# Input loads in three pieces, and a single line for the transfers in the scheduler's model

## The chip, the cores and the metric

The kernel runs on one core of one Trainium2 chip. The metric is device time in microseconds (us) of one launch, as the median of several runs. A core has a matmul engine (PE, whose weight loads are shown as PEld), a vector engine (DVE), an activation engine (ACT), GpSimd (POOL) and a sync engine (SP); here SP issues nearly all plain transfers and POOL the accumulating ones. Each engine runs its own instructions in the order in which the program has them, and waits at semaphores for the others.

## The reference

The input x has 32 images of 96 channels and 56 x 56 pixels, in float32. Two layers follow one another.

```python
# layer 0: an inverted bottleneck with 576 hidden channels
h = relu(bn(einsum('oc,bchw->bohw', w1, x)))
h = relu(bn(dwconv3x3(h, wdw)))
x = x + bn(einsum('oc,bchw->bohw', w2, h))
# layer 1 on tokens t (3136 of 96 channels)
h = relu(bn(einsum('bnc,hc->bnh', ln(t), a_w1)))        # 192 hidden
X = fft(h, axis=tokens)
xr = relu(X.real * rd - X.imag * id + rb)
xi = relu(X.imag * rd + X.real * id + ib)
t = t + bn(einsum('bnh,ch->bnc', ifft(xr + 1j * xi).real, a_w2))
t = t + qlinear(relu(qlinear(ln(t), W1, b1)), W2, b2)   # 384 hidden, operands rounded to 5+2 bit floats
```

The Fourier transform over 3136 tokens is done as matmuls with constant matrices, in two steps of 56.

## The kernel before

**The work.** An image is taken in two halves of 28 rows. For each half, `load_half` (line 586) brings 29 rows of x, 96 x 1624 numbers, into one of three buffers `xs`. Then come five groups of hidden channels. `last_channels` does the last 64 wholly on PE. `unit` (line 600) does each of the other four groups of 128 channels:

- PE expands it (line 617) and ACT evicts it to `hs` (line 627).
- ACT begins the depthwise sum in `acc` (line 643) with one tap and puts another tap into a buffer `product` (line 659). In units 1 and 3 (`DOUBLE`), a second tap goes into a second `product`.
- DVE adds the other taps to `acc`, one instruction each (line 670).
- POOL issues an accumulating transfer (line 678) that adds `product` to `acc`; in the double units one that adds the second product to the first comes before it.
- ACT applies the Relu to `acc` (line 687, `finish`), when that transfer has landed.

`front` (line 865) projects the half to token layout on PE (line 883), stores it for later (`tdr<-xt`, line 942), normalizes it and does the first step of the Fourier transform; the result goes to memory (`ydr<-ya`, line 1064). `mid` (line 1072), twice an image, loads it back the other way round (`yb<-ydr`, line 1094, and the matrix `wb`, line 1083), does the second step, the mixing and half of the inverse, and stores `gdr<-gc` (line 1275). `back` (line 1291), four times an image, loads the matrix `wd`, `gd<-gdr` and `tt<-tdr`, finishes the inverse, and does the normalization (its square root is line 837) and the quantized layers.

**What sets the order.** The order of the instructions on every engine is found while the program is built, by a small simulation, `Plan.emit` (line 223). Every piece of work is a `Step` with an engine, a cost in us, the steps that it comes after, the buffers that it takes and gives back, and a rank. Whenever an engine of the simulation is idle, it takes the ready step of lowest rank and writes its instructions into the program. A step's results count as there `late` us after its end. For a transfer, `late` is a tuple, and `Plan.moved` (line 200) works out when it lands. Before the change, it starts 1.4 us after its issue and takes its size over a rate (170 GB/s for loads and stores, 200 GB/s for the accumulating transfers) and an extra (1.5 us for loads, 3.0 for stores, 0 for accumulates), and the time for which it overlaps transfers already under way comes on top:

```python
        start = now + 1.4
        end = start + size / rate
        wait = sum(max(0.0, min(end, b) - max(start, a)) for a, b in self.moving)
        self.moving.append((start, start + 1.3 * size / rate))
        return end + wait + extra - now
```

On the chip the order is kept as it was written, and each instruction waits for what it really needs. So the times that the simulation assumes decide where an instruction stands, not when it may run. If PE would be idle in the simulation too long, a filler matmul (line 1491) is put in.

Of the kernel before, what the change touches and what calls it, by code (L numbers as in the profile page):

```python
# [41 lines left out]
C = 96  # L42
HD = 576
S = 56
# [8 lines left out]
W = R * S  # L53
XW = XR * S
# [74 lines left out]
PACE = {"last": 3.023, "front": 0.4, "mid": 0.54, "back": 0.45}  # L129
CHAIN = 0.6  # L130

SPARSE = 0.75
FILLER = 0.23
FIRST = 15.0
# [2 lines left out]
AT = (3.0, 0.5)  # L137
# [17 lines left out]
class Plan:  # L155
# [12 lines left out]
    def __init__(self, free):  # L168
        self.free = dict(free)
        self.steps = []  # L170
        self.now = self.pace = 0.0
        self.window, self.share, self.slow = 0, {}, False
        self.moving = []
        self.filler, self.recent = None, []

    def stretched(self, now, work):
# [22 lines left out]

    def moved(self, now, moves):  # L200

        size, rate, extra = moves
        start = now + 1.4
        end = start + size / rate
        self.moving = [m for m in self.moving if m[1] > start - 20]
        wait = sum(max(0.0, min(end, b) - max(start, a)) for a, b in self.moving)
        self.moving.append((start, start + 1.3 * size / rate))
        return end + wait + extra - now

    def job(self, now, pace):  # L210

# [2 lines left out]
    def step(self, engine, cost, emit, after=(), take=(), give=(), late=None, rank=None):  # L214
        late = self.LATE.get(engine, 0.1) if late is None else late
        if rank is None:
            rank = self.now
            self.now += self.pace
        s = Step(engine, cost, emit, list(after), list(take), list(give), late, rank, len(self.steps))
        self.steps.append(s)  # L220
        return s
# [62 lines left out]
def tile_kernel(ctx: ExitStack, tc: tile.TileContext, d: dict, out: bass.AP):  # L284
    nc = tc.nc
    nimg = d["x"].shape[0]
    x = d["x"].rearrange("i c a b -> i c (a b)")
# [60 lines left out]
    xs_ring = [cst([C, XW], f"xs{j}") for j in range(3)]  # L348
# [18 lines left out]
    def load(queue, o, src):  # L367
        queue.dma_start(out=o, in_=src)
        return o
# [73 lines left out]
    s = scale_of(vec[:, 0, :], vec[:, 3, :], 128, NK + 1)  # L443

    ps = psum()
    for k in range(NK + 1):
        j, at = divmod(128 * k, 512)
# [4 lines left out]
            start=True,  # L452
# [5 lines left out]
    s = scale_of(vec[:, 4, :], vec[:, 7, :], 128, NK + 1)  # L458
# [70 lines left out]
    def ffn():  # L529
# [6 lines left out]
        for o, v, p, n in ((b1q, fb, 128, 3), (b2q, fc, C, 1)):  # L536
# [4 lines left out]
    xs, acc, ydr, gdr, tdr = {}, {}, {}, {}, {}  # L541
    base = [0, R - 1]
# [3 lines left out]
    plan = Plan(  # L546
        {
            "ps": 3, "pw": 1, "hs": 3, "acc": 7, "product": 3, "hl0": 1, "hl1": 1, "al": 2,
            "xt": 1, "norma": 2, "brief": 3, "xnT": 1, "z": 2, "ya": 1, "wb": 1, "yb": 2,
            "V": 2, "eo": 3, "real": 1, "wd": 1, "gd": 1, "tt": 2, "normf": 2, "u8": 1, "uT": 1,  # L550
            "h8": 1, "h16": 2, "y16": 1, "ydr": 4, "gdr": 3, "tdr": 4,
        }
    )
    step = plan.step
# [7 lines left out]
    def dve(n, fixed=0.13):  # L562
        return fixed + n / 960

    def read(n):
        return n * 4, 170e3, 1.5

    def written(n):
        return n * 4, 170e3, 3.0

    bands_set = [step("DVE", 1.2, bands(j), rank=2.0 + j) for j in range(2)]
    sets = []
    for n, (f, count) in enumerate(((second, 7), (attention, 6), (mixer, 21), (ffn, 4))):
        t = step("SP", 0.55 * count, fetch, sets[-1:], late=(150e3, 170e3, 1.5), rank=-20.0 + n)
        sets.append(step("DVE", 3.0, f, sets[-1:] + [t], rank=14.0 + 4 * n))
    second_set, mixer_set, *mid_set = sets

# [6 lines left out]
    loaded, ready, strips, taken = {}, {}, {}, {}  # L584

    def load_half(img, s):
        n = 2 * img + s

        def load():
            xs[img, s] = xs_ring[n % 3]  # L590
            at = base[s] * S
            nc.sync.dma_start(out=xs[img, s][0:C, :], in_=x[img, :, at : at + XW])

        after = []
        if n >= 3:
            i, t = divmod(n - 3, 2)
            after = [taken[i, t], strips[i, t, "hl"]]
        loaded[img, s] = step("SP", 0.1, load, after, late=read(C * XW), rank=16 * n - 24)

    def unit(img, s, k):  # L600
        n = (2 * img + s) * NK + k
        o = R * s - base[s]
        up = 1 - 2 * s
        u = {}

        def weight(dr, dc):
            at = 3 * (dr + 1) + dc + 1
            return wdw[:, k, at : at + 1]

        def expand(h):  # L610
            def mm():
                if h == 0:
                    u["hs"] = w2.tile([128, XR, S], F32, name="hs", bufs=3)
                u[h] = psum()
                for j in range(2):
                    at = (2 * h + j) * QW
                    nc.tensor.matmul(  # L617
                        u[h][:, j, 0:QW],
                        lhsT=w1T[:, 128 * k : 128 * (k + 1)],
                        rhs=xs[img, s][0:C, at : at + QW],  # L620
                        start=True,
                        stop=True,
                    )

            def evict():
                flat = u["hs"].rearrange("p r c -> p (r c)")
                nc.scalar.activation(  # L627
                    flat[:, 2 * h * QW : 2 * (h + 1) * QW].rearrange("p (j w) -> p j w", j=2),
                    u[h][:, :, 0:QW],
                    AF.Relu,  # L630
                    bias=b1[:, k : k + 1],
                )

            after = [loaded[img, s]] if h == 0 else [u["first"]]
            e = u["first"] = step("PE", pe(QW, 128, 4), mm, after, ["ps"] + ["hs"] * (h == 0), rank=4 * n + OFF[0] + h)
            return step("ACT", act(2 * QW, 1), evict, [e], [], ["ps"], rank=4 * n + OFF[0] + h)

        e = [expand(0), expand(1)]

        def begin():  # L640

            acc[img, s, k] = w1.tile([128, R, S], F32, name="acc", bufs=7)
            nc.scalar.activation(  # L643
                acc[img, s, k],
                u["hs"][:, o + up : o + up + R, :],
                AF.Identity,
                scale=weight(up, 0),
                bias=bd[:, k : k + 1],
            )

        def span(dr, dc):

            return max(0, -(o + dr)), min(R, XR - o - dr), max(0, -dc), S - max(0, dc)

        def product(dr):
            def f():
                ra, rb, _, _ = span(dr, 0)
                u["p", dr] = w1.tile([128, R, S], F32, name="product", bufs=3)
                nc.scalar.activation(  # L659
                    u["p", dr][:, ra:rb, :], u["hs"][:, ra + o + dr : rb + o + dr, :], AF.Copy, scale=weight(dr, 0)  # L660
                )

            return f

        def tap(dr, dc):
            def f():
                ra, rb, ca, cb = span(dr, dc)
                src = u["hs"][:, ra + o + dr : rb + o + dr, ca + dc : cb + dc]
                dst = acc[img, s, k][:, ra:rb, ca:cb]
                nc.vector.scalar_tensor_tensor(dst, src, weight(dr, dc), dst, ALU.mult, ALU.add)  # L670

            return f

        def add(to, dr):
            def f():
                ra, rb, _, _ = span(dr, 0)
                t = acc[img, s, k] if to is None else u["p", to]
                nc.gpsimd.dma_start(  # L678
                    out=t[:, ra:rb, :].rearrange("p r c -> p (r c)"),
                    in_=u["p", dr][:, ra:rb, :].rearrange("p r c -> p (r c)"),  # L680
                    accum_op=ALU.add,
                )

            return f

        def finish():
            nc.scalar.activation(acc[img, s, k], acc[img, s, k], AF.Relu)  # L687

        t = step("ACT", act(W, 2, 0.09), begin, e, ["acc"], rank=4 * n + OFF[1])
        c = [step("ACT", act(W, 1, 0.09), product(0), e, ["product"], rank=4 * n + AT[0])]  # L690
        rest = [q for q in TAPS[1:] if q != (up, 0)]
        if k in DOUBLE:

            rest.remove((-up, 0))
            c.append(step("ACT", act(W, 1, 0.09), product(-up), e, ["product"], rank=4 * n + AT[1]))
        for at, q in enumerate(rest):
            last = q == rest[-1]
            t = step("DVE", dve(W - 28, 0.16), tap(*q), [t] + c * last, [], ["hs"] * last, rank=4 * n + OFF[2] + at * 3.5 / len(rest))
        if k in DOUBLE:
            c = [step("POOL", 1.0, add(0, -up), c, [], ["product"], late=(W * 128 * 4, 200e3, 0.0), rank=4 * n + AT[1])]  # L700
        t = step("POOL", 1.0, add(None, 0), [t] + c, [], ["product"], late=(W * 128 * 4, 200e3, 0.0), rank=4 * n + 3)
        ready[img, s, k] = step("ACT", act(W, 0, 0.09), finish, [t], rank=4 * n + OFF[3])

    def last_channels(img, s):
# [854 lines left out]
```

## Time and profile before

| | |
|---|---|
| time, median of 3 runs | 4589.91 us (4589.24 to 4595.37) |
| span of the profiled execution | 4584.2 us |
| mean granted PE clock | 0.988 |
| DMA queue of SP: share of 16 engines, MB | 36.2%, 479.15 |
| DMA queue of POOL: share of 16 engines, MB | 34.4%, 304.64 |
| accumulate onto `acc`, from issue to landing, median | 8.0 us (256 of them) |
| accumulate onto `product`, the same | 10.1 us (128 of them) |
| input loads `xs` | 64, of 609 KB each |

The profile is one execution. An engine's busy time is the time in which it executes; time in which it waits is idle time, and a view of waits says which engine's instruction, or which transfer, ended each. A group of instructions is named by its line in the kernel and by what it writes and reads. Transfers are shown at their issue; for the accumulating ones the landing is shown as well.

### The profile page before, as it was taken

To read this page: it belongs to the slowest core of one execution; us is meant where nothing else is said; L and a number is where in the kernel's file an instruction comes from. 1 tells how busy PE (TensorE), PEld (TensorE's weight loads), DVE (VectorE), ACT (ScalarE), POOL (GpSimd) and SP (SyncE) were. 2 spreads that over 40 slices of the span, in tenths; PEclk is the share of its full clock that TensorE was granted. 3 is DMA by queue.
4 is the path that set the end of the run, shared out by engine and by line. 5 is a ranking of instruction groups with operands and counts; after the bars stand their busy time and mean duration, and the time that the engine had idled before them with its cause. 6 is when DMAs were issued, how large, how long until landed. Compare 5 with 4: busy or idle time off the path is not lost.

```text
span 4584.2 us, 88412 instructions
## 1 busy us (share of the span) xinstructions
PE 4405.4 (96%) x35128; PEld 3296.1 (72%) x35128; DVE 4330.6 (94%) x7053; ACT 4114.5 (90%) x5390; POOL 340.7 (7%) x403
## 2 busy tenths in 40 slices
PE   8989999999999999999999999999999999999998
PEld 5667776777777777777777777777777777777777
DVE  8998999999999999999999999999999999999967
ACT  5677999999999999999999999999999999999965
POOL 1000000000000000000000000000000000000000
PEclk9999999999999999999999999999999999999999
DMA  4666777767767777767777767777767777767663
GB/s 104 135 155 157 190 171 176 187 162 185 181 163 188 174 179 185 184 166 191 173 176 185 183 163 188 174 176 183 187 162 188 174 174 190 179 165 191 168 170 107
DMA packets 390993, 789.44 MB, mean 172 GB/s; under 512 B 135696, under 2 KB 236628, under 8 KB 390580
## 3 DMA queue, kind: packets, MB, share of 16 engines
q1 hardware_dynamic: 335028, 479.15, 36.2%
q0 software_dynamic: 55488, 304.64, 34.4%
q8 instruction: 276, 4.52, 0.4%
q14 instruction: 137, 1.12, 0.1%
q10 hardware_dynamic: 64, 0.01, 0.0%
HBM read 286.38 MB, written 192.68 MB: 105 GB/s over the span
## 4 chain that ended last, share of the span: by engine, by line
PE 48%; ACT 22%; DVE 16%; DMA 8%; issue 4%; POOLq 0%; ACTq 0%; POOL 0%; SPq 0%; DVEq 0%
PE pw L883 11%; DVE acc L670 10%; PE ps L617 9%; DMA acc<-product 7%; PE ps L1005 4%; PE ps L1123 4%; PE ps L755 3%; PE ps L1036 3%; ACT product L659 3%; ACT hs L627 2%; ACT acc L687 2%; ACT acc L643 2%; PE ps L1329 2%; ACT h L1410 2%; ACT h L1395 2%
## 5 line engine op out<-in xcount | busy, mean ns | idle before, releaser
L670 DVE SCALAR_TENSOR_TENSOR acc<-hs,wdw,acc 128x1540 f32<-128x1540 f32 (+2 forms) x1664 | 2970.3, 1792 | 26.6 <-ACT acc L643 20.8
L617 PE MATMUL ps<-xs,w1T 96*128 96x406 f32 x2048 | 819.8, 523 | 24.6 <-ACT h L1395 16.7
L883 PEld LDWEIGHTS pw<-w2T,acc 128*112 128x112 f32 x7168 | 754.3, 178 | 62.1 <-issue 36.4
L883 PE MATMUL pw<-w2T,acc 128*112 128x96 f32 x7168 | 790.8, 264 | 4.5 <-ACT acc L687 4.5
L659 ACT ACTIVATE product<-hs,wdw 128x1568 f32<-128x1568 f32 (+1 forms) x384 | 613.8, 1599 | 21.6 <-DMA product<-product 20.9
L617 PEld LDWEIGHTS ps<-xs,w1T 96*128 96x128 f32 x2048 | 368.2, 194 | 261.7 <-issue 174.0
L627 ACT ACTIVATE hs<-ps,b 128x812 f32<-128x812 f32 x512 | 481.5, 941 | 51.2 <-PE ps L617 46.8
L687 ACT ACTIVATE acc<-acc 128x1568 f32<-128x1568 f32 x256 | 387.5, 1514 | 90.9 <-DMA acc<-product 85.1
L678 POOL DMA_DIRECT2D acc<-product x256 | 222.7, 870 | 3193.9 <-DVE mf L859 781.6
L643 ACT ACTIVATE acc<-hs,bd,wdw 128x1568 f32<-128x1568 f32 x256 | 437.0, 1707 | 0.3
L755 PE MATMUL ps<-hl,band 128*64 128x385 f32 (+3 forms) x3072 | 416.1, 495 | 0.3 <-ACT hs L627 0.3
L1005 PE MATMUL ps<-watt,xnT 97*120 97x192 f32 x1792 | 345.3, 337 | 60.9 <-DVE V L1152 59.6
L1005 PEld LDWEIGHTS ps<-watt,xnT 97*120 97x120 f32 x1792 | 299.0, 187 | 125.3 <-DVE V L1152 65.6
L1123 PEld LDWEIGHTS ps<-wb,yb 112*128 112x128 f32 x3528 | 297.3, 164 | 66.5 <-issue 20.9
L1395 ACT ACTIVATE h<-ps 128x784 f16<-128x784 f32 x384 | 319.6, 835 | 25.8 <-PE ps L1383 22.0
L1350 ACT ACTIVATE u<-tt,mf,rf 112x96 fp8e5<-112x96 f32 x812 | 312.3, 460 | 16.6 <-DVE mf L859 16.5
L1123 PE MATMUL ps<-wb,yb 112*128 112x112 f32 x3528 | 321.8, 271 | 4.4 <-ACT hs L627 2.6
L1410 ACT ACTIVATE h<-h 128x784 fp8e5<-128x784 f16 x348 | 301.9, 867 | 14.9 <-DVE h L1401 14.8
L755 PEld LDWEIGHTS ps<-hl,band 128*64 128x64 f32 (+1 forms) x3072 | 151.9, 134 | 198.9 <-issue 164.2
L1152 DVE SCALAR_TENSOR_TENSOR sb<-ps,cw,V 128x784 f32<-128x784 f32 x192 | 197.0, 1026 | 31.1 <-ACT V L1136 25.4
L1018 ACT ACTIVATE z<-ps 120x768 f32<-120x768 f32 (+1 forms) x256 | 182.3, 725 | 44.9 <-PE ps L1005 44.9
L1036 PE MATMUL ps<-z,wa 56*64 56x384 f32 (+1 forms) x2048 | 217.5, 496 | 0.3
(171 smaller groups left out, 6663.3 us busy)
## 6 DMA issues: line engine op xcount, KB each, us to landing
acc<-product POOLq DMA_DIRECT2D x256, 784.0 KB, 8.0
product<-product POOLq DMA_DIRECT2D x128, 756.0 KB, 10.1
yb<-ydr SPq DMA_DIRECT2D x252, 294.0 KB
wd<-in_wd_dram SPq DMA_DIRECT2D x128, 349.1 KB
wb<-in_wb_dram SPq DMA_DIRECT2D x63, 686.0 KB
ydr<-ya SPq DMA_DIRECT2D x256, 168.0 KB
xs<-in_x_dram SPq DMA_DIRECT2D x64, 609.0 KB
tdr<-xt SPq DMA_DIRECT2D x64, 588.0 KB
```

The costliest lines, as they stand in the source:

```text
L617: nc.tensor.matmul(u[h][:, j, 0:QW], lhsT=w1T[:, 128 * k : 128 * (k + 1)], rhs=xs[img, s][0:C, at : at + QW], start=True, stop=True,)
L627: nc.scalar.activation(flat[:, 2 * h * QW : 2 * (h + 1) * QW].rearrange("p (j w) -> p j w", j=2), u[h][:, :, 0:QW], AF.Relu, bias=b1[:, k ...
L643: nc.scalar.activation(acc[img, s, k], u["hs"][:, o + up : o + up + R, :], AF.Identity, scale=weight(up, 0), bias=bd[:, k : k + 1],)
L659: nc.scalar.activation(u["p", dr][:, ra:rb, :], u["hs"][:, ra + o + dr : rb + o + dr, :], AF.Copy, scale=weight(dr, 0))
L670: nc.vector.scalar_tensor_tensor(dst, src, weight(dr, dc), dst, ALU.mult, ALU.add)
L687: nc.scalar.activation(acc[img, s, k], acc[img, s, k], AF.Relu)
L755: nc.tensor.matmul(pv[:, :, ca:cb], lhsT=band[rows, j, dc + 1, 64 * o : 64 * o + 64], rhs=H[rows, q : q + 7, ca + dc : cb + dc], skip_grou ...
L883: nc.tensor.matmul(u["pw"][0:SK, t, n % 4, 0:C], lhsT=src[rows, (G * t + n) * SK : (G * t + n + 1) * SK], rhs=rhs, skip_group_check=True, **k,
L1005: nc.tensor.matmul(pv[0:PK, q - a, 0:HA], lhsT=xnT[:, q, 0:PK], rhs=watt, start=True, stop=True,)
L1123: nc.tensor.matmul(o, lhsT=lhsT, rhs=u["wb"][:, G * s + q, :], start=True, stop=True)
L1395: nc.scalar.activation(u["h", c].rearrange("p (j w) -> p j w", j=2), u["H", c][:, :, 0:n], AF.Copy)
L1410: nc.scalar.activation(u["h8"][:, c, :], u["h", c], AF.Copy, saturate=False)
```

## The change

It has two parts. First, an input load is cut by columns into three transfers of 560, 560 and 504 columns; in the simulation each of the second and third is issued when the one before it has landed. (The very first load stays whole.) The units may begin when the last piece has landed. It is meant to keep a large load from standing in the way of other transfers. Second, the simulation's model of transfers is replaced: all of them pass through one line at 225 GB/s, each begins at the earliest 1.0 us after its issue and when the one before it is through, and it counts as landed 0.5 us later, or 1.3 us later for the accumulating ones. With other landing times, the simulation may write another order for every engine. The work itself, its instructions and its buffers are the same except for the pieces.

```diff
+RATE = 225e3
+HARD = 0.5
+SOFT = 1.3
...
-        self.moving = []
+        self.moving = 0.0
...
     def moved(self, now, moves):
 
-        size, rate, extra = moves
-        start = now + 1.4
-        end = start + size / rate
-        self.moving = [m for m in self.moving if m[1] > start - 20]
-        wait = sum(max(0.0, min(end, b) - max(start, a)) for a, b in self.moving)
-        self.moving.append((start, start + 1.3 * size / rate))
-        return end + wait + extra - now
+        size, extra = moves
+        self.moving = max(self.moving, now + 1.0) + size / RATE
+        return self.moving + extra - now
+
+    def trickle(self, load, cuts, size, after, take, **k):
+
+        for n, (a, b) in enumerate(zip(cuts, cuts[1:])):
+            after = [self.step("SP", 0.1, load(a, b), after, take if n == 0 else [], late=(4 * size * (b - a), HARD), **k)]
+        return after[0]
...
     def read(n):
-        return n * 4, 170e3, 1.5
+        return n * 4, HARD
 
     def written(n):
-        return n * 4, 170e3, 3.0
+        return n * 4, HARD
...
-        t = step("SP", 0.55 * count, fetch, sets[-1:], late=(150e3, 170e3, 1.5), rank=-20.0 + n)
+        t = step("SP", 0.55 * count, fetch, sets[-1:], late=(150e3, HARD), rank=-20.0 + n)
...
-        def load():
-            xs[img, s] = xs_ring[n % 3]
-            at = base[s] * S
-            nc.sync.dma_start(out=xs[img, s][0:C, :], in_=x[img, :, at : at + XW])
+        def load(a, b):
+            def f():
+                xs[img, s] = xs_ring[n % 3]
+                at = base[s] * S
+                nc.sync.dma_start(out=xs[img, s][0:C, a:b], in_=x[img, :, at + a : at + b])
+
+            return f
...
-        loaded[img, s] = step("SP", 0.1, load, after, late=read(C * XW), rank=16 * n - 24)
+        cuts = [0, XW] if n == 0 else [0, 560, 1120, XW]
+        loaded[img, s] = plan.trickle(load, cuts, C, after, [], rank=16 * n - 24)
...
-            c = [step("POOL", 1.0, add(0, -up), c, [], ["product"], late=(W * 128 * 4, 200e3, 0.0), rank=4 * n + AT[1])]
-        t = step("POOL", 1.0, add(None, 0), [t] + c, [], ["product"], late=(W * 128 * 4, 200e3, 0.0), rank=4 * n + 3)
+            c = [step("POOL", 1.0, add(0, -up), c, [], ["product"], late=(W * 128 * 4, SOFT), rank=4 * n + AT[1])]
+        t = step("POOL", 1.0, add(None, 0), [t] + c, [], ["product"], late=(W * 128 * 4, SOFT), rank=4 * n + 3)
```

## The prediction, made before the changed kernel was run

> **What bounds the kernel now.** I read the page first, for the share of each engine.
>
> ```profile
> span 4584.2 us, 88412 instructions
> PE 4405.4 (96%) x35128; PEld 3296.1 (72%) x35128; DVE 4330.6 (94%) x7053; ACT 4114.5 (90%) x5390; POOL 340.7 (7%) x403
> ```
>
> Three engines are nearly full. PE's 4405.4 us hold 207.1 us of filler matmuls (line 1491), which do no work of the kernel, so DVE is the fullest engine: it has 4330.6 us of work, none of which the change touches, and 4584.2 - 4330.6 = 253.6 us of idle time. Any gain must come out of that. The view by windows says where it lies.
>
> ```profile
> core 0: us, PE busy (x) PEld busy (x) DVE busy (x) ACT busy (x) POOL busy (x), PEclk, DMA share, GB/s
> 0.00:400.00 400.00, 354.48 (x2531) 260.83 (x2532) 356.76 (x418) 261.17 (x267) 39.01 (x57) 0.94 0.61 137
> 400.00:4286.00 3886.00, 3770.90 (x30228) 2808.63 (x30228) 3743.65 (x6012) 3650.64 (x4837) 293.84 (x337) 0.99 0.73 178
> 4286.00:4585.00 299.00, 280.06 (x2377) 226.63 (x2373) 230.24 (x625) 202.72 (x287) 7.89 (x9) 1.00 0.55 143
> ```
>
> DVE idles 43.2 us at the start (18.5 of them before the first tap), 142.4 in the steady part and 68.8 at the end. The steady part repeats: 24 pairs of input loads take 138.1 us each, so an image has some 5 us of DVE idle time. The list of waits says on whom.
>
> ```profile
> ACT acc L687 <- DMA acc<-product: 85.1, 40, 5.1
> DVE rf L853 <- ACT sdf L837: 55.4, 62, 3.1
> ```
>
> DVE never waits for a DMA outside the set-up; it waits for ACT. ACT waits for a DMA 40 times at line 687, the Relu on a depthwise unit after its accumulating transfer. Those 40 have a pattern: from 400 us on there is one to an image, at the same place. Image 14, by the timelines of SP, POOL, ACT and DVE:
>
> ```profile
> 2009.31 0.43 SPq L592 DMA_DIRECT2D xs<-in_x_dram  x1
> 2010.76 0.32 SPq L942 DMA_DIRECT2D tdr<-xt  x1
> 2016.00 0.28 SPq L1301 DMA_DIRECT2D wd<-in_wd_dram  x1
> ```
>
> ```profile
> 2017.10 0.86 POOL L678 DMA_DIRECT2D acc<-product  x1 [14.74 <-DVE da L834]
> 2018.20 0.86 POOL L678 DMA_DIRECT2D product<-product  x1 [0.24 <-ACT product L659]
> ```
>
> ```profile
> 2026.64 1.51 ACT L687 ACTIVATE acc<-acc 128x1568 f32<-128x1568 f32 x1 [1.93 <-DMA acc<-product]
> 2028.05 0.19 ACT L837 ACTIVATE sdf<-wf 112x7 f32<-112x7 f32 x1
> ```
>
> ```profile
> 2028.28 0.20 DVE L853 RECIPROCAL rf<-sdf 112x7 f32<-112x7 f32 x1 [1.25 <-ACT sdf L837]
> ```
>
> The reader is to see a chain of four: a 609 KB input load and a 588 KB store go out 6 to 8 us ahead of an accumulate; the accumulate takes 9.52 us; ACT, in order, stands 1.93 us at line 687; the square root behind it comes late and DVE stands 1.25 us. Over all accumulates onto acc in the trace: 55 of the 64 input loads have one issued 6 to 9 us after them, and these take 9.4 us on average, while those 16 to 25 us after a load take 6.7 and those 25 to 40 us after it 6.0. Summing DVE's gaps within a DMA stall of ACT and the 3 us after it gives 41.8 us in the steady part, 156 us of it; at the rate elsewhere (2.7%) 4.2 us would be there. So the stalls cost DVE about 37.6 us, 1.3 us an image.
>
> **What the Trainium skill says.** "DMA: Bandwidth & Descriptors", section "Queues, rings and completion order", has each DMA engine go round the queues with work, a packet at a time. The trace agrees: between 2018 and 2027 us the packets of the accumulates and of the sync queue run side by side, 113 and 208 KB in the microsecond from 2019. The same page, "Issuing engines are not separate DMA queues", says that all issuers' transfers interleave on the same 16 engines, so a piece of an input load is still in an accumulate's way; only when it is put in changes. "PSUM — Partial Sum Buffer", section "Engine vs sequencer instructions", has the ACT and DVE queues as strict first-in first-out; the 1.93 us at line 687 that become 1.25 us of DVE show it.
>
> **The change, part by part.**
>
> 1. *Input loads in pieces.* 63 of 64 loads become three: 126 more transfers. Issuing one takes SP 0.43 us, so 126 x 0.43 = 54 us in all, 1.7 us an image. SP stands for hundreds of us on single lines (807.8 us for line 1314 alone), which hides it. Behind a waiting piece stand the other loads and stores of SP; pieces two and three wait for no buffer, only for their place in the order and one of SP's eight completion semaphores, which comes round after eight transfers (4584 us / 1770 of them x 8 = 20.7 us), against landings of 3 to 14 us. The rows shrink from 6,496 to 2,240 or 2,016 bytes; a 6,496-byte packet takes 247 to 384 ns in the trace, the nearest short one, 2,304 bytes, 93 ns, so three are some 280 ns, read from the trace's packet records: no cost. The last piece lands perhaps 10 us later than the one load did; a buffer of the ring of three comes free at rank 16n - 22.6 (the end of front n-3) and is first read at 16n - 4.5: 18 of the 32 ranks of an image, 18/32 of 138 us = 78 us. Hidden.
>
> 2. *What pieces bring.* When the accumulate of 2017.10 goes out, the sync queue still has work from the four yb loads, the input load, the store and wd. With pieces, the store goes ahead of the second and third, 409 KB. At the 250 GB/s moved there, 409 KB are 1.6 us, if neither has been issued by then, and 0.8 us if one has. ACT's stall of 1.9 us becomes 0.3 to 1.1 us.
>
> 3. *The order's model of DMA.* The order of all engines is fixed when the program is built, so a landing that is assumed wrongly becomes a wait. I put the old and the new formula over the transfers of the trace, in their order of issue. The trace's landing less the formula's, medians: product into product +3.1 us old, +1.0 new; product into acc +0.6 and +0.2; stores of ya, out and xt -2.5, -3.3 and -3.7 old, -0.2, -0.3 and -1.1 new; wb -2.1 and +0.3. So the new model is closer for most, and the spread is less for acc (1.3 to 1.0 us). The order will put line 687 of the double units later, behind the landing, and give back ya and the three "brief" tiles 2.5 to 3.3 us sooner. It gets worse for loads that PE waits for: yb +0.1 to +0.9, wd +0.6 to +1.9, gd -0.1 to +1.9. PE waits for none of them now, the buffers being filled long ahead, so I cost this at nothing.
>
> 4. *The start.* ACT's DMA stalls ahead of 400 us are 45 us, but SP is fetching weights and DVE waits mostly for the fill; I take 5 us of the 43.2.
>
> Sum: two thirds of 37.6 us (halfway between 0.3 and 1.1 us left of 1.9) is 25 us; 5 us at the start; 5 us of the other 100 us of steady idle time for buffers given back sooner, an estimate. 4590 - 35 = 4555 us.
>
> **The rivals.**
>
> *The whole order gets better.* Besides the stall, half of the 100 us goes: 4590 - 37 - 35 = 4518 us, with DVE at 98% in the steady part. For it: waits on ACT are what a wrong order makes. Against: the largest of them (line 837's and 1136's results) come from ACT's own costs, which stay as assumed.
>
> *Hidden or only moved.* Pieces two and three come out while the accumulate moves and take turns with it, so it lands as late as before: 4590 us. For it: the bytes are the same, and the trace shows the queues side by side. Against: the backlog ahead of the accumulate is shorter.
>
> *Slower: a new wait takes its place.* A piece now follows each landing, so two or three accumulates in a half may meet one, where one in an image stalled; or the shorter assumed landings of yb, wd and gd put a PE step ahead of its data. A stall such as today's costs 1.3 us x 31 = 40 us; one more than now gives 4630 us, and half a one 4610. For it: any change of assumed times deals the whole order anew, and 93% of ACT's and 96% of DVE's steady time is full. Against: the formulas fit better.
>
> **How the numbers follow.** Forecast 0.45 (4535 to 4575 us); better order 0.16; hidden 0.15, of which 0.03 falls to faster and 0.02 to slower; new wait 0.24. Faster by over 0.2% (under 4580.7): 0.45 + 0.16 + 0.03 = 0.64; within: 0.10; slower: 0.24 + 0.02 = 0.26. The range runs from 4505, a little beyond the better order, to 4625, most of one new stall an image; about 0.05 lies below and 0.12 above.
>
> **What would show it.** Right: the wait of ACT line 687 for the DMA falls from 85 us to under 40; no accumulate 6 to 9 us after an input piece takes over 9 us as a rule; product into product lands as before, near 10 us; DVE's steady idle time is 105 to 120 us at an unchanged 4330 us of work; the image's period is near 137 us. Wrong: line 687's wait as long as before at another place in the image; PE waiting for yb, wd or gd; DVE's waits for lines 837, 1136 and 1437 grown while the DMA wait shrank, which would mean that the new order, not the transfers, sets the time.

## The result and the profile after

The changed kernel takes 4565.05 us (median of 4 runs, 4560.63 to 4573.17) against 4589.57 us before: a ratio of 0.9948, 95% interval 0.9929 to 0.9968. That is 24.5 us or 0.5% faster; forecast were 35 us, to 4555, with a range of 4505 to 4625.

First the page of the changed kernel: the span, and the busy time of each engine.

```profile
span 4558.5 us, 88951 instructions
PE 4409.0 (97%) x35334; PEld 3306.1 (73%) x35334; DVE 4330.5 (95%) x7053; ACT 4118.9 (90%) x5390; POOL 341.6 (7%) x403
```

DVE's work is what it was, 4330.5 us against 4330.6. The whole difference of the spans, 4584.2 - 4558.5 = 25.7 us, is idle time of DVE. PE's work is not quite the same: the simulation wrote another number of filler matmuls, 1588 where 1382 stood, and these are the 206 more on PE. The view by windows of the changed kernel:

```profile
core 0: us, PE busy (x) PEld busy (x) DVE busy (x) ACT busy (x) POOL busy (x), PEclk, DMA share, GB/s
0.00:400.00 400.00, 367.23 (x2684) 270.43 (x2685) 365.96 (x430) 273.50 (x281) 39.32 (x58) 0.97 0.64 142
400.00:4286.00 3886.00, 3790.56 (x30483) 2827.55 (x30483) 3755.65 (x6049) 3663.87 (x4849) 296.14 (x339) 1.00 0.74 178
4286.00:4585.00 299.00, 251.20 (x2171) 208.14 (x2169) 208.85 (x576) 181.51 (x262) 6.18 (x7) 0.97 0.50 130
```

In the steady window DVE idles 3886.0 - 3755.7 = 130.3 us, where it was 142.4. Windows at fixed times cut the two programs at different work, so I also summed DVE's idle time up to equal amounts of DVE work: of the 25.6 us won, 13.6 come up to 400 us of work (images 1 to 3), 8.1 between 400 and 4100 us of work, and 3.9 in the end. An image takes 137.8 us, against 138.1 (images 4 to 30). The steady part has hardly moved. The waits of the changed kernel:

```profile
DVE h L1411 <- ACT h L1405: 54.0, 69, 6.4
ACT acc L697 <- DMA acc<-product: 41.9, 44, 2.7
DVE rf L863 <- ACT sdf L847: 22.6, 29, 2.4
```

Line numbers are 10 higher than before (7 for the input load). The wait that was to shrink did: ACT at its Relu waits 41.9 us for the accumulate where it waited 85.1, and DVE for the square root 22.6 where it waited 55.4. But other waits grew: DVE now waits 54.0 us at the quantized layer (44.5 before), and 16.7 us for PE in a step of `back`, where 5.8 stood. And the accumulates themselves land no sooner. The page's list of DMA issues, with the median time to landing last (8.0 and 10.1 us before):

```profile
acc<-product POOLq DMA_DIRECT2D x256, 784.0 KB, 8.9
product<-product POOLq DMA_DIRECT2D x128, 756.0 KB, 10.6
```

The old stall is also still there, once in three images. SP's timeline of the changed kernel near 2130 us, then POOL's, ACT's and DVE's:

```profile
2128.62 0.30 SPq L952 DMA_DIRECT2D tdr<-xt  x1
2128.97 0.43 SPq L599 DMA_DIRECT2D xs<-in_x_dram  x1
2133.86 0.28 SPq L1311 DMA_DIRECT2D wd<-in_wd_dram  x1
2134.18 0.31 SPq L599 DMA_DIRECT2D xs<-in_x_dram  x1
```

```profile
2134.71 0.86 POOL L688 DMA_DIRECT2D acc<-product  x1 [14.97 <-ACT pj L1245]
```

```profile
2144.39 1.51 ACT L697 ACTIVATE acc<-acc 128x1568 f32<-128x1568 f32 x1 [1.85 <-DMA acc<-product]
```

```profile
2146.03 0.20 DVE L863 RECIPROCAL rf<-sdf 112x7 f32<-112x7 f32 x1 [1.22 <-ACT sdf L847]
```

It is the chain of before with nearly the same sizes (1.85 and 1.22 us here, 1.93 and 1.25 before). The store went ahead of the piece as forecast, but the next piece goes out 0.5 us before the accumulate, which takes 9.66 us.

### The profile page after: what moved, and what is told of

It is laid out like the page before. It is cut to its first block, busy times and chain, and to the rows that moved or that the text cites. A ratio compares the mean times of both kernels' runs of the same rounds, so it can differ in the third digit from the quotient of the medians.

```text
span 4558.5 us, 88951 instructions
## 1 busy us (share of the span) xinstructions
PE 4409.0 (97%) x35334; PEld 3306.1 (73%) x35334; DVE 4330.5 (95%) x7053; ACT 4118.9 (90%) x5390; POOL 341.6 (7%) x403
## 4 chain that ended last, share of the span: by engine, by line
PE 39%; DVE 23%; ACT 22%; DMA 10%; issue 5%; SPq 0%; POOL 0%; POOLq 0%; DVEq 0%; ACTq 0%
DVE acc L680 15%; PE pw L893 11%; DMA acc<-product 8%; PE ps L627 6%; ACT acc L653 3%; ACT acc L697 3%; PE ps L1015 3%; ACT product L669 2%; PE ps L1133 2%; PE ps L1046 2%; PE ps L1339 2%; ACT hs L637 2%; ACT u L1360 2%; DVE sb L1162 1%; DMA gdr<-gc 1%
## 5 line engine op out<-in xcount | busy, mean ns | idle before, releaser
L627 PE MATMUL ps<-xs,w1T 96*128 96x406 f32 x2048 | 807.0, 517 | 22.8 <-ACT h L1405 9.1
L697 ACT ACTIVATE acc<-acc 128x1568 f32<-128x1568 f32 x256 | 387.5, 1514 | 47.9 <-DMA acc<-product 41.9
L1501 PE MATMUL pw<-ident 128*128 128x128 f32 x1588 | 228.5, 283 | 4.7 <-ACT xt L943 4.7
L1501 PEld LDWEIGHTS pw<-ident 128*128 128x128 f32 x1588 | 206.9, 195 | 30.2 <-issue 16.3
```

The source lines that it names most:

```text
L627: nc.tensor.matmul(u[h][:, j, 0:QW], lhsT=w1T[:, 128 * k : 128 * (k + 1)], rhs=xs[img, s][0:C, at : at + QW], start=True, stop=True,)
L1501: nc.tensor.matmul(pw[:, 0, 4 * C :], lhsT=ident, rhs=ident, start=False, stop=False, skip_group_check=True)
```

## The experiments

The theories. **A**: the transfers matter. Pieces clear the way for the accumulate behind an input load, and a closer model avoids waits. **B**: the new landing times write a better order, and the pieces are hidden. **C**, formed after the first four runs: any small change of the assumed times writes the whole order anew, as cards are dealt anew (below such an order is called a deal), and the deal sets the time. Medians and ratios to before, in the order of the runs:

| run | us | ratio, 95% interval |
|---|---|---|
| the changed kernel | 4565.05 | 0.9948, 0.9929 to 0.9968 |
| e1 pieces, old model | 4548.50 | 0.9914, 0.9900 to 0.9928 |
| e2 new model, whole loads | 4484.38 | 0.9774, 0.9761 to 0.9788 |
| e3 changed order, whole loads | 4570.18 | 0.9960, 0.9948 to 0.9973 |
| e4 order of before, little input | 4527.73 | 0.9870, 0.9855 to 0.9884 |
| e5 changed kernel at 220 GB/s | 4496.41 | 0.9790, 0.9772 to 0.9808 |
| e6 changed kernel at 230 GB/s | 4625.91 | 1.0074, 1.0052 to 1.0096 |
| e7 e2 at 220 GB/s | 4635.40 | 1.0092, 1.0074 to 1.0111 |
| e8 e2 at 230 GB/s | 4655.87 | 1.0137, 1.0119 to 1.0155 |
| e9 order of before, pieces | 4600.63 | 1.0024, 1.0016 to 1.0032 |
| e10 order of e2, pieces | 4482.43 | 0.9765, 0.9753 to 0.9778 |
| e11 changed kernel, two pieces | 4476.28 | 0.9756, 0.9743 to 0.9769 |
| e12 changed kernel, accumulates 0.5 us later | 4507.71 | 0.9822, 0.9809 to 0.9836 |

**Each part alone (e1, e2).** In e1 `moved` and its numbers stay as before and the load is cut; against the kernel before:

```diff
+            after = [self.step("SP", 0.1, load(a, b), after, take if n == 0 else [], late=(4 * size * (b - a), 170e3, 1.5), **k)]
...
-        loaded[img, s] = step("SP", 0.1, load, after, late=read(C * XW), rank=16 * n - 24)
+        cuts = [0, XW] if n == 0 else [0, 560, 1120, XW]
+        loaded[img, s] = plan.trickle(load, cuts, C, after, [], rank=16 * n - 24)
```

> Three pieces, with the old model of landings (170 GB/s, 1.5 us). Theory A (the pieces clear the way for the accumulate that follows an input load): the wait of ACT for the accumulate at the Relu falls from 85 us to under 45, and the time to about 4565 us. Theory B (what counts is the new order that the new landing times write, and the pieces are hidden): another order without the better landing times, so no gain to be counted on: 4580 to 4620 us.

In e2 the model is the new one and the load stays whole; against the changed kernel:

```diff
-        cuts = [0, XW] if n == 0 else [0, 560, 1120, XW]
+        cuts = [0, XW]
```

> The new model of landings with whole input loads. Theory A: the accumulates that follow a whole load still take over 9 us and stall ACT; the wait at the Relu is near 80 us and the time 4580 to 4595 us. Theory B: the gain is here, 4555 to 4575 us, with the start (the first three images) shorter by some 13 us of DVE idle time as in the changed kernel.

Each part alone is faster than both together: 41 us and 105 us won, 24.5 together. A's sign for e1 came out (the Relu's wait is 26.2 us), but its e2 didn't: whole loads, and the wait is 31.0 us. B fares no better: e2 was 71 us faster than B's range, its start is 8 us shorter and not 13, and the changed kernel, which is e2 with pieces and the order that comes of them, is 81 us slower than e2. Effects that don't add up like this speak against both. The waits of e2:

```profile
DVE h L1411 <- ACT h L1405: 84.6, 97, 6.4
ACT acc L697 <- DMA acc<-product: 31.0, 24, 5.4
```

Most of DVE's idle time in e2's steady part (58 us) sits in one kind of wait, at the quantized layer. The waits for the square root (2.9 us, 55.4 before) and for the begun sum (3.4, 20.8 before) are all but gone. The view by windows of e2, columns as above, has DVE idle for 70.5 of 3850 us:

```profile
400.00:4250.00 3850.00, 3800.91 (x30565) 2815.36 (x30564) 3779.54 (x6110) 3687.07 (x4906) 297.66 (x343) 1.00 0.76 182
```

**The same order, other transfers (e3, e4).** e3 keeps the order of the changed kernel on all engines and moves the whole load in the first piece's place:

```diff
-                nc.sync.dma_start(out=xs[img, s][0:C, a:b], in_=x[img, :, at + a : at + b])
+                if a == 0: nc.sync.dma_start(out=xs[img, s][0:C, :], in_=x[img, :, at : at + XW])
```

> Every engine's order exactly as in the changed kernel, but the whole input load is issued in the place of the first piece and the places of the other two are empty. It isolates what the pieces do on the chip. Theory A: the wait of ACT at the Relu rises from 42 us to 65 or more, and the time by 10 to 25 us, to 4575 to 4590. Theory B: the time stays within 5 us of the changed kernel's 4565.

It takes 4570.18 us, 5.1 more than the changed kernel, with intervals that overlap: on the chip, three pieces or one is no difference to be told here. The Relu's wait is not 65 us:

```profile
ACT acc L697 <- DMA acc<-product: 45.7, 41, 5.5
```

So A fails here, and B, which allowed 5 us, holds but for a hair. e2 and e3 both issue whole loads, and 86 us lie between them: what differs is the order, with the fillers in it (1286 and 1588).

e4 keeps the order of before and takes the load away, nearly:

```diff
-            nc.sync.dma_start(out=xs[img, s][0:C, :], in_=x[img, :, at : at + XW])
+            nc.sync.dma_start(out=xs[img, s][0:C, 0 : XW if n < 3 else S], in_=x[img, :, at : at + (XW if n < 3 else S)])
```

> The order of before exactly; from the fourth half image on, an input load brings only the first 56 of 1624 columns (the rest of the half is computed on old columns). It takes the load out of the accumulate's way altogether and so measures the most that the contention can cost. Theory A: the wait at the Relu falls from 85 us to under 30 and the time by about 38 us, to 4552. Theory B: the accumulate still waits for the store and the other loads, or DVE's time comes back in other waits: less than 15 us, 4575 to 4590.

62 us won, more than A's 38, although the Relu's wait fell only to 46.3:

```profile
ACT acc L687 <- DMA acc<-product: 46.3, 37, 4.6
DVE rf L853 <- ACT sdf L837: 23.0, 45, 2.7
```

The windows of before, then of e4, leave DVE 141.9 and 91.5 us idle of 3850:

```profile
400.00:4250.00 3850.00, 3734.90 (x29913) 2780.21 (x29913) 3708.09 (x5964) 3615.78 (x4791) 291.26 (x334) 0.99 0.73 178
400.00:4250.00 3850.00, 3769.25 (x30332) 2804.24 (x30334) 3758.55 (x6057) 3662.66 (x4856) 295.45 (x339) 1.00 0.72 172
```

So in the order of before the load's traffic does cost: DVE waits 23.0 us for the square root where it waited 55.4. Whether pieces spare any of it is what e9 asks.

But the accumulates themselves hardly gained. Those issued 6 to 9 us after a load take 8.8 us on average in e4, where they took 9.4, though the load now brings 56 columns of 1624. The trace of before shows what else is beside them: all 55 run together with an accumulating transfer of product into product, and of the 64 accumulates 16 to 40 us after a load only two do. The accumulates more than 40 us after any load take 9.3 us too: 10.0 with such a transfer beside them, 8.5 without. So the prediction's comparison (9.4 us against 6.7 and 6.0) set accumulates that have a second accumulating transfer beside them against accumulates that have none, and put the difference down to the load. About 0.6 us of it is the load's bytes. No run moved the transfer of the products.

**The deal (e5 to e8).** One number is changed, the assumed rate, to 220 or 230 GB/s, with pieces (e5, e6) and with whole loads (e7, e8):

```diff
-RATE = 225e3
+RATE = 220e3
```

> The changed kernel with an assumed rate of 220 instead of 225 GB/s: nothing changes but the order that the simulation writes. Theory A (the time follows from how well the model fits the transfers): 2% of the rate is within the fit's error, so 4565 us within 10. Theory C (the order is dealt anew by any small change of the assumed times, and the deal sets the time): it lands anywhere in 4490 to 4620 us, and differs from 4565 by 15 us or more.

> The changed kernel with an assumed rate of 230 GB/s. Theory A: 4565 us within 10. Theory C: anywhere in 4490 to 4620 us, by 15 us or more from 4565, and not on one line with the run at 220.

> The new model with whole loads (4484 us at 225 GB/s), with 220 GB/s. Theory A: within 10 us of 4484, as whole loads would be better than pieces under this model. Theory C: 4484 was a lucky deal: 4510 to 4600 us.

> The new model with whole loads, with 230 GB/s. Theory A: within 10 us of 4484. Theory C: 4510 to 4600 us, at the upper end, since the simulation's own end with this rate is 58 us later than with 225 (4532 against 4474).

Theory A fails in all four runs. Theory C holds in the main: all four lie far outside A's 10 us. Its ranges were too narrow, though: e6, e7 and e8 are slower than C had them (4620 and 4600 at most). With pieces, 220, 225 and 230 GB/s give 4496, 4565 and 4626 us, which is close to one line, against C's forecast; with whole loads they give 4635, 4484 and 4656, which is not. A change of 2% in one assumed number moves the time by 61 to 171 us, while all instructions but the fillers are the same. The changed kernel less the one with whole loads, at the three rates, is -139, +81 and -30 us, which is no effect of pieces. The waits of e8, the slowest:

```profile
DVE h L1411 <- ACT h L1405: 100.4, 58, 6.4
ACT acc L697 <- DMA acc<-product: 80.6, 53, 4.0
DVE eo L1177 <- ACT V L1168: 48.1, 35, 3.1
DVE tt L1344 <- DMA tt<-tdr: 30.7, 13, 4.6
```

Besides the Relu's stall it has DVE waiting for a load, `tt`, 13 times: a step has been put ahead of its data, as the prediction feared for PE. Its windows leave DVE 212.5 us idle of 3850:

```profile
400.00:4250.00 3850.00, 3738.39 (x29891) 2797.85 (x29889) 3637.47 (x5853) 3540.24 (x4696) 287.32 (x328) 0.99 0.73 175
```

**Pieces without a new deal (e9, e10).** The orders of PE, DVE, ACT and POOL are kept; only SP issues a piece after each of its next two steps:

```diff
+LATER = []
...
-                    s.emit()
+                    n = LATER[:1] if s.engine == "SP" else []; s.emit(); [LATER.remove(f) or f() for f in n]
...
-            nc.sync.dma_start(out=xs[img, s][0:C, :], in_=x[img, :, at : at + XW])
+            part = lambda a, b, t=xs[img, s]: nc.sync.dma_start(out=t[0:C, a:b], in_=x[img, :, at + a : at + b]); part(0, 560 if n > 2 else XW); LATER.extend([lambda: part(560, 1120), lambda: part(1120, XW)] if n > 2 else [])
```

> The orders of PE, DVE, ACT and POOL exactly as before; only SP's changes: from the fourth half image on, the load goes out in three pieces, the second after SP's next step (mostly the store of xt), the third after the one that follows (mostly wd or gdr). It is step 2 of the prediction by itself: the accumulate 6 to 9 us after the load should take 8 us instead of 9.4, the wait of ACT at the Relu should fall from 85 us to 50 or less, and the time by about 25 us, to 4565 us. If the bytes only move beside the accumulate (the rival): 4585 to 4595 us and the wait stays at 75 to 85.

> The same for the order of the new model with whole loads, 4484 us, whose accumulates seldom stall ACT (7 us in the steady part): if the pieces act only through the accumulate's stall, there is nothing to win here, 4480 to 4486 us; if loads in the way cost something else too, 4470 us or less.

e9 missed on the far side: 4600.63 us, 0.24% slower than before, and the Relu's wait has grown. Its waits:

```profile
ACT acc L687 <- DMA acc<-product: 108.8, 62, 4.8
DVE rf L853 <- ACT sdf L837: 77.6, 64, 3.2
```

SP's timeline of e9 at one of the stalls, and POOL's:

```profile
1325.27 0.32 SPq L942 DMA_DIRECT2D tdr<-xt  x1
1325.63 0.42 SPq L592 DMA_DIRECT2D xs<-in_x_dram  x1
1330.51 0.28 SPq L1301 DMA_DIRECT2D wd<-in_wd_dram  x1
1330.83 0.31 SPq L592 DMA_DIRECT2D xs<-in_x_dram  x1
```

```profile
1331.61 0.86 POOL L678 DMA_DIRECT2D acc<-product  x1 [14.75 <-PE ps L1252]
```

The store goes ahead of the second piece, but the third piece goes out 0.8 us before the accumulate and is in flight beside it. The accumulates issued 6 to 9 us after a transfer of input take 10.05 us on average (9.37 before); 8 were expected. (The profiled execution of e9 took 4609.33 us and that of before 4585.98, further apart than the medians, so not all of the difference of the waits is the pieces'.) In e10, where the order has few such stalls, the pieces change nothing: 4482.43 against 4484.38 us. Pieces by themselves thus cost 10 us in one order, and in two others gained 5 (e3) and 2 us (e10), neither to be told from nothing.

**Picking a deal (e11, e12).** The simulation that writes the order has an end of its own. It is no time of the chip, but it can be had for each order: 4489 for before and for the changed kernel, 4517 for e1, 4474 for e2, and 4478, 4492, 4494 and 4532 for e5 to e8. The two fast kernels had the lowest. Two orders with low ends were therefore run, both from the changed kernel:

```diff
-        cuts = [0, XW] if n == 0 else [0, 560, 1120, XW]
+        cuts = [0, XW] if n == 0 else [0, 812, XW]
```

> The changed kernel with the load in two pieces (812 columns each), so a new deal; the simulation ends it at 4470 us, earlier than any other (4474 with whole loads and 4489 with three pieces at 225 GB/s; the two fast kernels so far have 4474 and 4478, all those at 4489 and more measured 4548 to 4656). If the simulation's own end tells a good deal from a bad one: 4475 to 4500 us. If not, anywhere in 4490 to 4640.

```diff
-SOFT = 1.3
+SOFT = 1.8
```

> The changed kernel with accumulates assumed to land 1.8 instead of 1.3 us after the line (in the changed kernel's trace they land 1.0 us later than assumed onto acc and 1.75 later onto product). The simulation ends it at 4472.5 us. If its end tells the deal: 4475 to 4500 us; if a closer fit counts as well, under 4484. If neither: anywhere in 4490 to 4640.

e11 at 4476.28 us is the fastest of all, 1.9% under the changed kernel. e12 at 4507.71 is 8 us outside what was expected of a good deal, so the closer fit of the accumulates' landing was no help. Over the ten orders written by the simulation, its end and the chip's time correlate with 0.72; the four under 4480 measured 4476 to 4508 us, the six above 4548 to 4656. Within a group the end says little: e1 has the second latest end and is the fastest of the six.

**PE's clock in these orders.** No run was made for this, but the traces show it. Each trace records the share of full speed at which PE was allowed to run. Here it is 1 or 0.5: in the kernel before, a matmul of line 617 takes 504 ns in the median at the one and 882 ns at the other. Image 14 of the kernel before, whose stall at 2026.6 us the prediction followed, goes on like this (columns as above, the clock third from the end):

```profile
2037.71:2041.12 3.41, 1.75 (x8) 1.46 (x9) 3.41 (x4) 2.55 (x6) 0.00 (x0) 1.00 0.68 206
2041.12:2044.53 3.41, 3.41 (x18) 2.58 (x17) 3.41 (x5) 3.41 (x5) 0.00 (x0) 0.50 0.00 0
```

PE waits 2.14 us for a result of DVE (line 1152), is busy for 1.75 of 3.41 us, and then runs 3.41 us at half speed. That wait is the longest in total in PE's list, before and in the changed kernel:

```profile
PE ps L1005 <- DVE V L1152: 59.6, 29, 2.1
PE ps L1015 <- DVE V L1162: 29.2, 29, 2.1
```

Between 400 and 4286 us, the kernel before has 14 stretches at half speed, each right after 3.4 us in which PE was busy for 37 to 54%. The changed kernel and e1 have 2; e3 and e4 7; e6 12, e8 13, e7 and e9 22; e2, e5, e10 and e11 none and e12 one. So the five kernels under 4510 us have at most one, and the five over 4589 us have twelve or more. Over the ten orders written by the simulation, the whole time at half speed (111 us before, 46 in the changed kernel) correlates with the chip's time at 0.87. (`Plan.stretched` in the kernel models such stretches, and the fillers are put in where the simulated PE is idle; the change left both as they were.) What comes first is not shown: PE stands idle in part ahead of each stretch in the kernel before, but no run changed the clock or the number of fillers alone. It isn't all of the time either: e2 and the changed kernel both have 46 us at half speed, and 81 us lie between them.

## Why the prediction was right, and where it wasn't

- *The bound.* Right: DVE's work stayed at 4330.5 us, and the gain is idle time of DVE.
- *Step 1, 126 more transfers at no cost.* SP's issuing is hidden, as e10 shows (4482 against 4484 us). That the pieces cost nothing was too much said: in the order of before they cost 10 us (e9).
- *Step 2, the pieces take the Relu's stall from 1.9 us to 0.3 to 1.1 us, worth 25 us.* This is the step that failed as a mechanism. e9 does just that in the order of before, and the wait rose from 85.1 to 108.8 us. The sign that was named for it failed as well: in the changed kernel the accumulates 6 to 9 us after a transfer of input take 9.5 us on average, where none was to take over 9 as a rule. I had counted the store as moved ahead of 409 KB and granted that a piece might have been issued by then, but not that the third piece would fall right before the accumulate. The rival "hidden or only moved" described it, and so did the Trainium skill ("DMA: Bandwidth & Descriptors", section "Issuing engines are not separate DMA queues"): the engines are shared whoever issues, so a cut changes when bytes are in the way and not how many. e9 agrees, with 10.05 us where 9.37 stood. The same meeting stands in the changed kernel's trace (2134.18 and 2134.71 us). And there was less to win than thought: with nearly all of the load's bytes gone (e4), these accumulates still take 8.8 us.
- *The stalls cost DVE 1.3 us an image.* Supported, but only in the order of before: with the load's bytes gone (e4) 62 us come back, more than the 37.6 counted, so the load costs in other places as well, or the count near the stalls missed some of it (PE's stretches at half speed, 7 in the steady part instead of 14, were not in it). In the changed kernel the wait at the Relu fell by 43 us and the steady part won only 8.1, while waits at other lines grew.
- *Step 3, a closer model gives a better order, 5 us.* The size isn't a size at all: orders of the new model range from 4476 to 4656 us. The fit is closer, as said; that closeness makes the order better is not shown, and three of its eight orders are slower than before.
- *Step 4, the start.* 5 us were forecast; 13.6 were won by 400 us of DVE's work, the largest single part of the gain. It comes with the new order: e3, with whole loads in that order, has 12.5 us of it. In both, PE is at half speed for 24 of the first 400 us, where it was for 44 before. And a reading was wrong: of the 18.5 us up to DVE's first tap, DVE is idle for only 6.8, as it does set-up work for the rest.
- *The rival "a new wait takes its place"* gave the true reason, "any change of assumed times deals the whole order anew", and times of 4610 to 4630 us. e6, e7 and e8 are that case, with 4626 to 4656 us. That the changed kernel's deal fell on the faster side of before isn't explained by anything in the prediction.
- *The rival "the whole order gets better"* has a slip in its sum: half of 100 us is 50, so it stood for 4503 us and not 4518. e5 and e2, at 4496 and 4484, went further still.

So the sum came out near by parts that were each off: 25 us expected of the stalls in the steady part, where it won 8; 5 at the start, where it won 14. That it did is luck: of the eight orders that the new model wrote, only the changed kernel and e12 lie in the range that was forecast, 4505 to 4625 us. What stays open is what makes one order good. The sum of ACT's stalls on DMA from 400 to 4286 us goes with the time over eight orders (before, changed, e1, e2, e5 to e8: correlation 0.78), but e5 is fast at 36 us of it and e1 slower at 13, and no run changed these stalls alone with everything else kept. PE's time at half speed goes with the time more closely, but it too was never changed alone.

## What to carry to other kernels

Where a program writes a fixed order from assumed times, try an edit of the assumptions beside its neighbours, a few per cent up and down, before believing its gain: here one edit gave 0.5%, and its neighbours (e5 to e8) spread from 4496 to 4656 us, 3.5%. To learn what a transfer or a cut does on the chip, keep every engine's order and change the transfer alone; three such runs (e3, e9, e10) showed 0.24% at most. And once the spread is known, it is worth more than the edit: choose among orders, with the scheduler's own end as a coarse sieve and the chip as the judge. When a time is compared between transfers that do and don't have something ahead of them, look at what else goes with it: here a second accumulating transfer stood beside every one of the slow 55.

## What the runs showed of the hardware that was not expected

DVE's busy time isn't fixed by its instructions. In every kernel that does the whole work DVE has the same 7053 instructions. Their durations add up to 4847.8 us before and 4839.9 in e2, but the time that they cover is 4330.6 and 4308.5 us. Neighbouring records overlap (in e9's trace an instruction of 0.17 us starts at 1339.48 and the next at 1339.57), and what they cover goes with the order: 4308 to 4312 us in the five fast kernels (e2, e5, e10, e11, e12), 4327 to 4337 in all others. The sums of the durations don't go with it: e10, in e2's order, has 4849.4 us of durations and covers 4308.7. The 22 us between before and e2 are a part of the 104 us between their spans.

A small transfer right before an accumulate was no better for it than a large one 6 to 9 us earlier: 10.05 us on average with 504 columns some 0.7 us ahead (e9), 9.4 us with 1624 columns 6 to 9 us ahead (before). Both have an accumulating transfer of the products beside them.

A wait of PE can cost more than its own length. All 14 stretches at half clock in the steady part of the kernel before, 3.4 or 6.8 us long, came right after 3.4 us with PE busy for 37 to 54%. One of 3.4 us costs some 1.5 us of PE's time on top of the wait, an estimate from the 882 ns that a matmul took there and the 504 that it took otherwise.
